# Transposes of x1 moved from TensorE to VectorE blocks and SBUF-to-SBUF transfers, with the order of a pass rearranged

## The chip, the cores and the metric

The kernel runs on one core of one Trainium2 chip. The metric is the device time of one execution in microseconds. Engines are named as in the profile: PE (TensorE), DVE (VectorE), ACT (ScalarE), POOL (GpSimd), SP (SyncE, which only issues transfers here).

## The reference

An input x of 2 x 4096 x 256 (float32) goes through one gated recurrence and one feed-forward block, each with a layer norm behind it:

```python
u = x @ W_in + b_in;  g = sigmoid(x @ W_gate + b_gate)
h_t = tanh(h_prev @ A + u_t @ Bm)            # a scan over 4096 steps
y_t = g_t * (h_t @ C.T + u_t @ D.T) + (1 - g_t) * x_t
x1  = layernorm(x + (y @ W_out + b_out + x))
h   = gelu(x1 @ bw1.T + b1)                  # 256 -> 1024, exact gelu
out = layernorm(x1 + (h @ bw2.T + b2))       # 1024 -> 256
```

bw1 and bw2 are the weights' signs times the mean magnitude of a row. The sums of the feed-forward block are kept exact to float32 by splitting x1 and h into a high part (float32r) and the remainder, `hi` and `lo`, and multiplying both with the signs.

## The kernel before, in words

Each of the two sequences is cut into 64 segments that run side by side (with 48 warm-up steps, and a comparison at the end that proves the segments' joints), so the recurrence takes 48 + 64 steps. A step is one product on PE and one tanh on ACT (`steps`, L156), strewn between the other work. The tokens are handled in 16 chunks of 512 (4 blocks of 128 tokens, 256 features).

The order of PE, ACT, DVE and POOL is written out by hand inside `tc.manual_schedule`: a sequence of `do(chunk, stage)` calls emits each stage's instructions on each engine, and an engine runs its own in that order. SP is not among these engines before, so its transfers are ordered by the compiler's scheduler.

A chunk goes through these stages:

- `load` (L342): its h and u are gathered from `st` into `hu` by two SBUF-to-SBUF transfers, its x into `xn`.
- `gate`, `tanh` (L357, L360): the gate's product, and a tanh on ACT into `tg`.
- `mix`, `mix_end` (L365, L380): the product `ps_y` on PE; POOL adds `b_out` to `xn` in four instructions (`add_row`, L353, with `bo_r`); DVE makes `d` (L377, L382) and then y in place of `tg` (L385).
- `project` (L388), in two halves: y times W_out on PE into `ps_z`; behind the second half DVE's addition into `xn`, which from here on is x1 (L406), and its statistics `bs_a`, `mv_a`, `rs_a`; POOL raises `rs_a` to the power -1/2 (L266).
- `shift`, `norm` (L410, L414): `nm_a` on DVE (L271), and the normalization in four instructions on ACT (L279).
- `turn` (L418): eight 128x128 transposes on PE into PSUM (`ps_t`, L423), `hi` copied by ACT (L431), `lo` subtracted by DVE (L433).
- `rest` (L437): POOL adds `b2` to x1 (L355, `b_r`).
- `up` g, for g = 0 to 3 (L442): eight products into two banks, two gelus (L458) and a rounded copy `hhi` (L467) on ACT. `low` g (L470): `hlo` on DVE (L474).
- `down` g (L532): 16 products with the second weights into `ps_o` (L490); behind g = 3 DVE scales it into `o` (L506).
- `add`, `stats`, `store` (L510 to L521): x1 + o on DVE (L512), statistics `bs_b`, `mv_b`, `rs_b`, POOL's power, normalization (L281, four instructions on DVE), and the transfer to `out`.

One pass c of the main loop (L723) works on several chunks, in this order on PE: up 0 of chunk c; down 2 of chunk c-1; mix of c+2; up 1; down 3 of c-1; a piece of the later chunks' gates (passes 1 to 12); turn of c+1; up 2; down 0; the first half of the projection of c+2; up 3; down 1; its second half. PSUM is full: three banks `h` for up and gates, two for `ps_y`, `ps_z` and `ps_t` in turn, two for `ps_o`, one for the recurrence. Tiles named with `bufs=` are reused in turn, and a reuse waits for the last reader.

Of the kernel before, what the change touches and what calls it, by code (L numbers as in the profile page):

```python
# [8 lines left out]
FP = mybir.dt.float32  # L9
FR = mybir.dt.float32r  # L10
# [6 lines left out]
P = 128  # L17
B, T, DM, S, H = 2, 4096, 256, 64, 1024
KD = DM // P
# [4 lines left out]
N = 512  # L24
# [3 lines left out]
TB = N // P  # L28
# [9 lines left out]
def gated_recurrence_then_binary_ffn(  # L38
# [16 lines left out]
    nc = tc.nc  # L55
# [3 lines left out]
    wk = ctx.enter_context(tc.tile_pool(name="work", bufs=2))  # L59
# [40 lines left out]
    def load_xT(c, pieces=1):  # L100
        x_tiles[c] = xp.tile([P, KD, N], FP, tag="xt", name=f"xt{c}", bufs=XTB)
        for k in range(pieces):
            cut = slice(k * KD // pieces, (k + 1) * KD // pieces)
            nc.sync.dma_start(out=x_tiles[c][:, cut, :], in_=xT[c][:, cut, :])
# [224 lines left out]
    class Chunk:  # L329


        def __init__(self, c, name, at=lambda a, c: a[c]):
            self.c, self.nm, self.at, self.xt = c, name, at, None

        def load_x(self):
            self.xt = xp.tile([P, KD, N], FP, tag="xt", name=f"xt_{self.nm}", bufs=XTB)
# [5 lines left out]
        def load(self):  # L342
            c, nm = self.c, self.nm
            self.hu = xp.tile([P, N], FP, tag="hu", name=f"hu{nm}", bufs=3)
            for r, src in (
                (TOP, h_of[:, bass.ds(c * SPC + 1, SPC)]),
                (LOW, u_of[:, bass.ds(c * SPC, SPC)]),
            ):
                nc.sync.dma_start(out=self.hu[r, :], in_=src.rearrange("p j b k -> p (j b k)"))
            self.xn = xp.tile([P, TB, DM], FP, tag="xn", name=f"xn{nm}", bufs=4)  # L350
            nc.sync.dma_start(out=self.xn, in_=self.at(x, c))

# [12 lines left out]
        def mix(self):  # L365

            nm, xt_ = self.nm, self.xt
            ps = p_m.tile([P, KD, N], FP, tag="m", name=f"ps_y{nm}")
            for m in range(KD):
                nc.tensor.matmul(  # L370
                    ps[:, m, :], cd[:, bass.ts(m, P)], self.hu, start=True, stop=True
                )
                if m < KD - 1:
                    yield
            self.add_row(self.xn, bo_r)
            self.d = wk.tile([P, KD, N], FP, tag="y", name=f"d{nm}", bufs=1)
            nc.vector.tensor_sub(self.d, ps, xt_)  # L377
            yield

# [38 lines left out]
        def turn(self, apart=False):  # L418
# [15 lines left out]
            self.h = {}  # L434
            yield

        def rest(self):  # L437

            self.add_row(self.x1, b2_r)
            yield  # L440

        def up(self, g, apart=False):  # L442
            nm = f"{self.nm}_{g}"
            h = wk.tile([P, 2, N], FP, tag="h", name=f"h{nm}")
            hi = wk.tile([P, 2, N], FR, tag="hhi", name=f"hhi{nm}", bufs=3)
            self.h[g] = h, hi
            for i in range(2):
                j = 2 * g + i
                ps = p_1.tile([P, N], FP, tag="h", name=f"ps_h{nm}_{i}")
                for n, (k, part) in enumerate((k, p) for p in (self.hi, self.lo) for k in range(KD)):  # L450
                    nc.tensor.matmul(  # L451
                        ps,
                        sg1[:, k, bass.ts(j, P)],
                        part[:, k, :],
                        start=n == 0,
                        stop=n == 2 * KD - 1,
                    )
                nc.scalar.activation(  # L458
                    h[:, i, :],
                    ps,  # L460
                    AF.Gelu,
                    bias=b1_c[:, j : j + 1],
                    scale=al1[:, j : j + 1],
                )
                if i == 1:
                    for part in range(2) if apart else [slice(0, 2)]:
                        nc.scalar.copy(hi[:, part, :], h[:, part, :])  # L467
                yield
# [41 lines left out]
        def add(self, blocks=range(TB), engine=nc.vector):  # L510
            cut = slice(blocks[0], blocks[-1] + 1)
            engine.tensor_tensor(  # L512
                self.x1[:, cut, :], self.x1[:, cut, :], self.o[:, cut, :], ALU.add
            )
            yield
# [68 lines left out]
        def redo(self):  # L584

            self.load_x()
            self.load()
            pieces = [self.gate, self.mix, self.mix_end, lambda: self.project(0), lambda: self.project(1)]
            pieces += [self.shift, self.norm, self.turn, self.rest]
            for g in range(KH // 2):  # L590
                pieces += [lambda g=g, f=f: f(g) for f in (self.up, self.low, self.down)]
            for piece in pieces + [self.add, self.stats, self.store]:
                for _ in piece():
                    pass


    ch = [Chunk(c, f"{c}") for c in range(NC)]
# [34 lines left out]
    def step():  # L632
        if ready():
            next_steps()

    def do(i, what, *args, pace=5600):
        if not 0 <= i < len(ch):
            return
        if what == "load":
            need = WARM + (ch[i].c + 1) * SPC  # L640
            while done < need:
                next_steps()
            ch[i].load()
        elif what in ("load_x", "load_gate_x"):
            getattr(ch[i], what)()
        else:
            emit(what, getattr(ch[i], what)(*args), pace)
# [4 lines left out]
        emit("part", (next(early, None) for _ in range(n)), pace)  # L652

    ET = mybir.EngineType
    with tc.manual_schedule(engines={ET.PE, ET.Activation, ET.DVE, ET.Pool}):
        waiting = []
        for c in range(FIRST + 1, FIRST + 6):
            load_xT(c)
# [5 lines left out]
        for n, pair in enumerate(pairs):  # L664
            before = 2 if n == 0 else 1
            parts(before, EARLY)
            if pair:
                emit("", u_of_chunks(*pair))
                if pair == (13, 14):
                    emit("", u_of_chunks(15, 0))  # L670
                emit("u", [None], EARLY)
            for c in loads[n]:
                load_xT(c)
            if n == 0:
                load_weights()
            if n == 3:
                halve_weights()
            if n >= 5:
                load_xT(n + 3)
            for i in range(7 - before):  # L680
                if 1 <= n < 5 and i == 0:
                    load_w(n - 1)
                if 2 <= n < 6 and i == 3:
                    prepare_w(n - 2)
                parts(1 if (n, i) != (6, 5) else 0, EARLY)
# [33 lines left out]
        end = len(ch) - 1  # L719
        parts_met = compare()  # L720
        since = -1 << 40
        late = gates(ch[10:], TB)
        for c in range(end):  # L723
            do(c + 6, "load_x")
            if c % 2 == 0:
                do(10 + c // 2, "load_gate_x")
            do(c, "up", 0)
            do(c, "low", 0)
            step()
            do(c - 1, "down", 2)  # L730
            do(c + 3, "load")
            if c > 0:
                do(c + 1, "shift")
                do(c + 1, "norm")
                do(c + 2, "mix")
                do(c + 2, "mix_end")
            do(c, "up", 1)
            step()
            do(c - 1, "down", 3)
            def add():  # L740
                do(c - 1, "add", range(TB), nc.gpsimd if c == end - 1 else nc.vector)
                if c < end - 1:
                    do(c - 1, "stats")

            if 1 <= c <= 12:
                add()
                emit("gate", (next(late, None) for _ in range(KD)))
            do(c + 1, "turn")
            do(c, "low", 1)
            if not 1 <= c <= 12:  # L750
                add()
            do(c + 1, "rest")
            do(c, "up", 2)
            do(c, "low", 2)
            if c == end - 1:
                do(c - 1, "stats")
            else:
                do(c - 1, "store")
            if c == end - 2:
                assert done == len(plan), done  # L760
                next(parts_met)
                next(parts_met)
            step()
            do(c, "down", 0)
            do(c + 2, "project", 0)
            do(c, "up", 3)
            step()
            do(c, "down", 1)
            do(c, "low", 3)
            if c == end - 1:  # L770
                do(c - 1, "store")
            do(c + 2, "project", 1)
            if c == end - 2:
                next(parts_met)
                next(parts_met)
        count()
        do(end, "up", 0)
        do(end, "low", 0)
        do(end - 1, "down", 2)
        do(end - 1, "down", 3)  # L780
# [76 lines left out]
```

## Time and profile before

| | |
|---|---|
| median of 3 runs | 451.37 us (451.14 to 454.42) |
| the profiled execution | 451.76 us |
| its span, first to last instruction | 450.0 us |
| mean granted TensorE clock | 0.994 |
| transfers issued by SP in one pass | 4 or 5 |

The span of the profile is cut from the first instruction to the last; what lies around it makes the 1.76 us to the execution's time. A row of a timeline is start, duration, engine, line, operation, output<-inputs and count; rows of the chain of work that ended last are start, duration, and what ran. "Idle before" names what the engine waited for. In rows of DVE two successive instructions may overlap by some 0.08 us[...].

The main loop's passes, by the chain: 23.41 us each for c = 1 to 10, 22.7 for c = 11 and 12 (the recurrence is over by then), 20.89 for c = 13 (no gate) and 17.45 for c = 14; chunk 15's own feed-forward takes the last 27.35 us.

### The profile page before, as it was taken

The page shows a single profiled execution, that of the slowest core. Times are in us where ns is not written, and L with a number is a line of the kernel's source. Part 1 is how long each engine was busy: PE and PEld are TensorE (multiplying, and loading weights), DVE is VectorE, ACT ScalarE, POOL GpSimd, SP SyncE. Part 2 cuts the span into 40 slices and gives each one's busy share as a digit, 9 for nine tenths or more (in the row PEclk, how much of TensorE's full clock was granted, in tenths as well). Part 3 has the DMA queues.
Part 4 walks back from the last instruction along what each step waited for, and adds up shares of the span by engine and source line. Part 5 has one row for each costly group of instructions (what it writes and reads, how often), then busy time and mean ns, then how long its engine had stood idle before and what let it go on. Part 6 is the DMA issues. An engine that isn't in the chain of part 4 may idle for free.

```text
span 450.0 us, 6729 instructions
## 1 busy us (share of the span) xinstructions
PE 438.2 (97%) x2506; PEld 355.6 (79%) x2506; DVE 357.4 (79%) x597; ACT 259.9 (58%) x424; POOL 177.6 (39%) x177
## 2 busy tenths in 40 slices
PE   8999999999999999999999999999999999999992
PEld 5665766788888888887979797979788888897982
DVE  0245927967979797989898889899898989887774
ACT  2443541585656574847474747566666656565771
POOL 1001300643545454545445454545454545433413
PEclk9999999999999999999999999999999999999997
DMA  8997824221133313331331313111202020201013
GB/s 298 306 320 289 290 67 134 69 86 23 48 108 104 108 58 106 105 106 58 105 106 61 105 60 105 61 58 50 70 20 87 1 93 1 93 1 48 1 47 101
DMA packets 14838, 44.51 MB, mean 99 GB/s; under 512 B 2000, under 2 KB 3024, under 8 KB 14800
## 3 DMA queue, kind: packets, MB, share of 16 engines
q1 hardware_dynamic: 14224, 43.65, 29.2%
q8 instruction: 22, 0.36, 0.4%
q10 hardware_dynamic: 576, 0.37, 0.3%
q14 instruction: 16, 0.13, 0.1%
HBM read 31.43 MB, written 8.39 MB: 88 GB/s over the span
## 4 chain that ended last, share of the span: by engine, by line
PE 86%; DVE 6%; DMA 3%; ACT 3%; issue 1%; POOL 1%; SPq 0%; POOLq 0%; DVEq 0%
PE ps_h L451 24%; PE ps_o L490 23%; PE ps_z L395 12%; PE ps_g L313 11%; PE ps_y L370 6%; PE ps_s L157 5%; PE ps_u L131 3%; PE ps_t L423 3%; DMA xt<-in_xT 3%; DVE hlo L474 1%; ACT xn L279 1%; ACT h L458 1%; DVE xn L281 1%; DVE bs_a L256 1%; ACT hhi L467 1%
## 5 line engine op out<-in xcount | busy, mean ns | idle before, releaser
L458 ACT ACTIVATE h<-ps_h,bias_c,al 128x512 f32<-128x512 f32 x128 | 97.4, 776 | 86.3 <-PE ps_h L451 80.3
L490 PE MATMUL ps_o<-sg,hhi 128*128 128x256 f32 x496 | 121.3, 285 | 0.0
L490 PE MATMUL ps_o<-sg,hlo 128*128 128x256 f32 x496 | 117.9, 279 | 0.1
L474 DVE TENSOR_TENSOR hlo<-h,hhi 128x1024 fp32r<-128x1024 f32 (+1 forms) x65 | 83.7, 1305 | 23.1 <-ACT hhi L467 23.0
L490 PEld LDWEIGHTS ps_o<-sg,hlo 128*128 128x128 f32 x496 | 93.5, 188 | 1.1 <-DVE hlo L474 0.3
L490 PEld LDWEIGHTS ps_o<-sg,hhi 128*128 128x128 f32 x496 | 93.5, 189 | 0.8
L451 PE MATMUL ps_h<-xhi,sg 128*128 128x512 f32 x256 | 91.8, 440 | 0.0
L355 POOL TENSOR_TENSOR xn<-xn,bo_r 128x256 f32<-128x256 f32 x64 | 65.4, 1052 | 48.4 <-DMA xn<-in_x 48.4
L451 PE MATMUL ps_h<-xlo,sg 128*128 128x512 f32 x256 | 80.1, 394 | 0.2
L355 POOL TENSOR_TENSOR xn<-xn,b_r 128x256 f32<-128x256 f32 x64 | 70.8, 1134 | 2.0 <-PE ps_t L423 2.0
L467 ACT CAST hhi<-h 128x1024 fp32r<-128x1024 f32 (+1 forms) x65 | 67.3, 1037 | 2.0
L313 PE MATMUL ps_g<-xt,w_gate 128*128 128x384 f32 (+3 forms) x208 | 66.3, 430 | 0.2 <-DMA xt<-in_xT 0.2
L266 POOL TENSOR_TENSOR rs_a<-rs_a,neg_half 128x4 f32<-128x4 f32 x16 | 17.2, 1075 | 121.3 <-DVE rs_a L265 96.6
L395 PE MATMUL ps_z<-w_out,tg 128*128 128x256 f32 x256 | 60.7, 380 | 0.0
L158 ACT ACTIVATE st<-ps_s 64x128 f32<-64x128 f32 x112 | 30.1, 269 | 47.6 <-PE ps_s L157 47.1
L451 PEld LDWEIGHTS ps_h<-xlo,sg 128*128 128x128 f32 x256 | 48.1, 188 | 11.8 <-DVE xlo L433 0.9
L451 PEld LDWEIGHTS ps_h<-xhi,sg 128*128 128x128 f32 x256 | 46.6, 189 | 13.4 <-issue 6.2
L157 PEld LDWEIGHTS ps_s<-st,wab 128*128 128x128 f32 x224 | 38.5, 188 | 22.2 <-ACT st L158 10.0
L266 POOL TENSOR_TENSOR rs_b<-rs_b,neg_half 128x4 f32<-128x4 f32 (+1 forms) x17 | 19.2, 1132 | 87.9 <-PE ps_s L157 49.9
L395 PEld LDWEIGHTS ps_z<-w_out,tg 128*128 128x128 f32 x256 | 46.1, 189 | 5.1
L279 ACT ACTIVATE xn<-xn,nm_a,rs_a 128x256 f32<-128x256 f32 x60 | 31.2, 591 | 26.5 <-DVE nm_a L271 26.5
L157 PE MATMUL ps_s<-st,wab 128*128 128x128 f32 x224 | 43.9, 278 | 0.1
(73 smaller groups left out, 483.5 us busy)
## 6 DMA issues: line engine op xcount, KB each, us to landing
xt<-in_xT SPq DMA_DIRECT2D x35, 512.0 KB, 4.2
xn<-in_x SPq DMA_DIRECT2D x16, 512.0 KB, 3.4
out_y<-xn SPq DMA_DIRECT2D x15, 512.0 KB, 2.6
hu<-st SPq DMA_DIRECT2D x32, 128.0 KB, 2.2
w1t<-in_w1T SPq DMA_DIRECT2D x2, 512.0 KB, 5.6
w1n<-in_w SPq DMA_DIRECT2D x2, 512.0 KB, 6.3
w2t<-in_w2T SPq DMA_DIRECT2D x2, 512.0 KB, 4.7
xt<-in_xT SPq DMA_DIRECT2D x2, 256.0 KB, 3.4
```

Source lines behind the costliest of these rows:

```text
L157: nc.tensor.matmul(p_h, ab, st[:, j].rearrange("p b k -> p (b k)"), start=True, stop=True)
L158: nc.scalar.activation(h_of[:, j + 1].rearrange("p b k -> p (b k)"), p_h[TOP, :], AF.Tanh)
L266: nc.gpsimd.tensor_tensor(rs, rs, neg_half[:, cut], ALU.pow)
L279: nc.scalar.activation(r, r, AF.Identity, bias=self.sh[:, i : i + 1], scale=rs)
L313: nc.tensor.matmul(ps[:, cut], w_gate[:, k, bass.ts(m, P)], xt_[:, k, cut], start=k == 0 and i == 0, stop=k == KD - 1, skip_group_check=True,)
L355: nc.gpsimd.tensor_tensor(r[:, i, :], r[:, i, :], row, ALU.add)
L395: nc.tensor.matmul(self.ps_z[:, i, :], self.y[:, k, bass.ts(i, P)], w_out[:, k, :], start=k == 0, stop=k == KD - 1,)
L451: nc.tensor.matmul(ps, sg1[:, k, bass.ts(j, P)], part[:, k, :], start=n == 0, stop=n == 2 * KD - 1,)
L458: nc.scalar.activation(h[:, i, :], ps, AF.Gelu, bias=b1_c[:, j : j + 1], scale=al1[:, j : j + 1],)
L467: nc.scalar.copy(hi[:, part, :], h[:, part, :])
L474: nc.vector.tensor_sub(lo[:, i, :], h[:, i, :], hi[:, i, :].bitcast(FP))
L490: nc.tensor.matmul(ps[:, i, :], part[:, j % 2, bass.ts(tb, P)], sg2[:, j, :], start=j == 0 and part is self.h[j // 2][0] and first, stop=j ...
```

## The change

For chunks 2 to 14 the transposes on PE are replaced: `blocks` turns x1 in 32x32 blocks by one DVE instruction into a new tile `xb`, and 16 SBUF-to-SBUF transfers on SP put the blocks in their places in `lo`. The tokens then stand in another order inside a chunk, which the gelu undoes as it writes h (a rearranged output). `split`, called between the two gelus of up 3 of the chunk before, makes `hi` (ACT) and the remainder `lo` (DVE, in place). Chunks 0, 1 and 15 keep `turn`.

The order of a pass changes as well. `shift` and `norm` of c+1 go to its head, then `low` 3 of c-1 (which stood at the end of the pass before), then `blocks`; `turn`, where it is left, keeps its place. Both halves of the projection of c+2 stand ahead of up 3, so its addition and statistics on DVE do too. The normalization of `store` is done by ACT (with a shift `nm_b` on DVE, as in `shift`), and stands between up 2 and `low` 2. `load` is split, with `load_n` for x; SP joins the engines whose order is written out by hand. `d` takes the buffer of `o`. In up 0 to 3 the products are as they were.

```diff
+        def blocks(self):
+            nm, Q = self.nm, P // 32
+            xb = wk.tile([P, DM // 32, TB, 32], FP, tag="xb", name=f"xb{nm}", bufs=1)
+            nc.vector.transpose(
+                out=xb, in_=self.x1.rearrange("p i (b r) -> p b i r", r=32)
+            )
+            self.lo = wk.tile([P, KD, N], FR, tag="xlo", name=f"xlo{nm}")
+            for a in range(Q):
+                for q in range(Q):
+                    nc.sync.dma_start(
+                        out=self.lo.bitcast(FP)[bass.ts(q, 32), :, bass.ts(a, P)],
+                        in_=xb[bass.ts(a, 32), q :: Q, :, :].rearrange("p k i c -> p k (i c)"),
+                    )
+            yield
+
+        def split(self):
+            self.hi = wk.tile([P, KD, N], FR, tag="xhi", name=f"xhi{self.nm}")
+            nc.scalar.copy(self.hi, self.lo.bitcast(FP))
+            nc.vector.tensor_sub(self.lo, self.lo.bitcast(FP), self.hi.bitcast(FP))
+            self.h = {}
+            self.far = True
...
-        def up(self, g, apart=False):
+        def up(self, g, apart=False, between=None):
...
+                to = h[:, i, :]
+                if self.far:
+                    to = to.rearrange("p (i a c) -> p a i c", a=P // 32, c=32)
                 nc.scalar.activation(
-                    h[:, i, :],
-                    ps,
+                    to,
+                    ps.rearrange("p (a i c) -> p a i c", a=P // 32, c=32) if self.far else ps,
...
+                if i == 0 and between is not None:
+                    between()
...
-    with tc.manual_schedule(engines={ET.PE, ET.Activation, ET.DVE, ET.Pool}):
+    with tc.manual_schedule(engines={ET.PE, ET.Activation, ET.DVE, ET.Pool, ET.SP}):
...
         for c in range(end):
+            far = 0 < c < end - 1
+            if c > 0:
+                do(c + 1, "shift")
+                do(c + 1, "norm")
+                do(c - 1, "low", 3)
+                if far:
+                    do(c + 1, "blocks")
+            do(c, "up", 0)
+            step()
+            do(c - 1, "down", 2)
+            if c > 0:
+                do(c + 2, "mix")
+                do(c + 2, "mix_end")
+            do(c, "low", 0)
+            do(c + 3, "load")
             do(c + 6, "load_x")
             if c % 2 == 0:
                 do(10 + c // 2, "load_gate_x")
-            do(c, "up", 0)
-            do(c, "low", 0)
-            step()
-            do(c - 1, "down", 2)
-            do(c + 3, "load")
-            if c > 0:
-                do(c + 1, "shift")
-                do(c + 1, "norm")
-                do(c + 2, "mix")
-                do(c + 2, "mix_end")
...
-            do(c + 1, "turn")
+            if not far:
+                do(c + 1, "turn")
...
             do(c, "up", 2)
+            if c < end - 1:
+                do(c - 1, "store", range(TB), nc.scalar)
+                do(c + 3, "load_n")
             do(c, "low", 2)
             if c == end - 1:
                 do(c - 1, "stats")
-            else:
-                do(c - 1, "store")
...
             do(c, "down", 0)
             do(c + 2, "project", 0)
-            do(c, "up", 3)
+            do(c + 2, "project", 1)
+            do(c, "up", 3, False, ch[c + 1].split if far else None)
             step()
             do(c, "down", 1)
-            do(c, "low", 3)
...
-            do(c + 2, "project", 1)
...
         do(end, "up", 0)
+        do(end - 1, "low", 3)
```

## The prediction

> **What bounds the kernel now.** I read the busy shares first, then the chain of work that ended last, then that chain inside one pass of the main loop, then DVE's and POOL's timelines beside it, and last SP's queue.
>
> ```profile
> PE 438.2 (97%) x2506; PEld 355.6 (79%) x2506; DVE 357.4 (79%) x597; ACT 259.9 (58%) x424; POOL 177.6 (39%) x177
> ```
>
> PE is busy nearly always; DVE has a fifth free on average, but not evenly. One pass of the main loop, from the chain:
>
> ```profile
> 221.79 1.85 PE ps_h L451 x8
> 223.64 0.22 PE ps_s L157 x2
> 223.86 1.83 PE ps_o L490 x16
> 225.70 1.72 PE ps_y L370 x4
> ...
> 231.31 1.72 PE ps_g L313 x4
> 233.03 0.87 PE ps_t L423 x8
> ...
> 245.20 0.94 PE ps_h L451 x4
> ```
>
> A pass is 245.20 - 221.79 = 23.41 us, all PE, with no wait in it. The eight transposes of `turn` are 0.87 us of it: the only PE work that the change takes away. In the table of stretches DVE is busy 20.93 us of these 23.41, so DVE has 2.5 us left. DVE's rows around it, then POOL's:
>
> ```profile
> 213.57 2.88 DVE L474 TENSOR_TENSOR hlo<-h,hhi 128x1024 fp32r<-128x1024 f32 x2
> 216.37 2.65 DVE L281 TENSOR_SCALAR xn<-xn,mv_b,rs_b 128x256 f32<-128x256 f32 x4
> ...
> 226.72 0.68 DVE L271 SCALAR_TENSOR_TENSOR nm_a<-mv_a,rs_a 128x4 f32<-128x4 f32 x1
> 227.45 1.23 DVE L377 TENSOR_TENSOR d<-ps_y,xt 128x1024 f32<-128x1024 f32 x1
> ...
> 250.12 0.16 DVE L271 SCALAR_TENSOR_TENSOR nm_a<-mv_a,rs_a 128x4 f32<-128x4 f32 x1
> ```
>
> ```profile
> 213.66 4.88 POOL L355 TENSOR_TENSOR xn<-xn,b_r 128x256 f32<-128x256 f32 x4
> ...
> 226.11 4.42 POOL L355 TENSOR_TENSOR xn<-xn,bo_r 128x256 f32<-128x256 f32 x4
> ```
>
> While POOL adds rows, a DVE instruction with two SBUF inputs takes longer: two `hlo` 2.88 instead of twice 1.22, `nm_a` 0.68 instead of 0.16. It works the other way too (DVE, then POOL, at the end of the run):
>
> ```profile
> 400.73 1.22 DVE L474 TENSOR_TENSOR hlo<-h,hhi 128x1024 fp32r<-128x1024 f32 x1
> ...
> 425.24 1.38 DVE L281 TENSOR_SCALAR xn<-xn,mv_b,rs_b 128x256 f32<-128x256 f32 x4 [0.91 <-POOL rs_b L266]
> ```
>
> ```profile
> 400.97 1.86 POOL L266 TENSOR_TENSOR rs_b<-rs_b,neg_half 128x4 f32<-128x4 f32 x1 [7.97 <-DVE rs_b L265]
> ```
>
> POOL's power, 1.02 elsewhere, came behind an `hlo` that ended at 401.95 and ended itself 0.88 later. And L281 x4 costs 1.38 with POOL idle, 2.65 beside its adds: the two engines take turns.
>
> **What the skill says.** "SBUF — State Buffer", section "Who interferes with whom": DVE instructions with two SBUF inputs and POOL instructions that read SBUF exclude one another for a whole instruction, and a DVE instruction with one SBUF input is free of it. The trace agrees: `d<-ps_y,xt` (one input in PSUM) stays at 1.23 beside POOL. "VectorE: DVE Perf Modes", section "The three transpose paths": DVE transposes within 32x32 blocks only, so the transfers must place the blocks. "Perfetto Trace Analysis", section "Identifying Dependency Chains": an instruction with many waits gets wait instructions in front of it; in this trace such ones stand 0.10 us apart.
>
> **The change, part by part.**
>
> *Taken away:* 0.87 us of PE in chunks 2 to 14, 13 x 0.87 = 11.3 us if PE stays the bound; L281 on DVE (2.65 a pass), which ACT does instead as in L279 (2.08 for four). ACT goes from 14.6 to 16.7 busy in a pass of over 22, which hides it; its `xhi` now reads SBUF, as `hhi` does (1.05 for 1.01).
>
> *DVE's transpose:* no row. The skill's "Vector Engine (DVE) Microarchitecture Reference", section 3.8, has one element per cycle and lane, so 1024 elements cost as the 1024-wide rows here: 1.22. It is issued behind `norm`, which ends near 2.5 us into a pass (`lo` at 0.27, `nm_a` 0.2, `norm` 2.08), and DVE's next, `d`, waits for `ps_y` until 5.66. Below 3.1 us it is free, above it every us counts.
>
> *16 transfers a chunk on SP:* nearest are the `hu` transfers, SBUF to SBUF:
>
> ```profile
> 63.66 1.13 SPq L349 DMA_DIRECT2D hu<-st  x2
> ```
>
> 0.58 apart, and 2.2 us to landing in the page's list. So 3.8 + 15 x 0.58 + 2.2 = 14.7 us into the pass, needed at about 20.8: free up to 0.98 us each. Bounds 0.33 (an `xt` load) to 1.2 (double); at 1.2 they come 3 us late. ACT's `xhi` waits for all of them, and behind it on ACT stand the second gelu of up 3, `hhi` 3 and the next `norm`. Behind the transfers on SP stand `hu`, `xt`, the store and `xn`, all with most of a pass to spare. `xn` waits for the store to land, and so lands some 2 us into the next pass; POOL's `bo_r` adds then run from 2.2 to 5.2, where DVE has nothing on the path.
>
> *The loop that closes.* Before, `hi` and `lo` of the next chunk were made in mid-pass, far ahead. Now `split` makes them inside the last up group; `lo`'s subtraction stands on DVE behind the projection's addition and statistics, and the next pass's up 0 needs it at its third matmul. PE then waits on DVE, and DVE's `d` on PE. I walk round this loop, times from start to start in the rows.
> 1. `lo` ends to `d` starts: `d` starts 227.45 - 221.79 = 5.66 behind up 0; `lo` must have ended 0.27 behind it (the row of the first `xlo` matmul stands at 222.10, less 0.04 for the signal). 5.39.
> 2. DVE without a gap: d 1.26, L382 1.26, L385 1.14, `hlo` 0 1.14, o 1.25, add 1.25, bs_b 1.33, mv_b 0.40, rs_b 0.08, `hlo` 1 1.22: 10.33. Everything these wait for is there earlier (the last is down 3, by 9.7 against `o` at 10.5).
> 3. The new `nm_b` stands between `hlo` 1 and `hlo` 2 and waits for POOL's power, which is shut out by `hlo` 1 and ends 0.90 behind it. POOL then starts its four b_r adds (0.75 alone); `nm_b` comes behind the first (0.75), `hlo` 2 behind the second (0.70) and runs 1.12. To the addition L410: 3.47.
> 4. L410 1.25, bs_a 1.33, mv_a 0.40, rs_a 0.45 (0.08 and four wait instructions for the 16 transfers), `lo` 1.22: 4.65.
> Sum 5.39 + 10.33 + 3.47 + 4.65 = 23.84, against 22.54 (23.41 - 0.87) for PE alone. PE then idles some 1.3 us a pass.
>
> *Sum over the run* (passes before from the chain): c = 1 to 10, 23.84 - 23.41 = 0.43, ten times 4.3. c = 11 and 12, where the recurrence is over: 23.62 (0.22 less in 1) against 22.70, twice 0.92 = 1.8. c = 13, without a gate, was 20.89 on PE; the DVE loop does not shrink, and the comparison adds 0.5: 24.1, so 3.2. c = 14 was 17.45 because the chain waited for the norm of chunk 15; now that comes first, and PE's own work is 4 x 3.67 + 0.87 + 0.12 = 15.7: -1.75. Start: the lower half of `hu` now follows the upper one in SP's order, 0.6 to 0.7 later in a chain that holds it: 0.7. Together +8.3: span 458.3 for 450.0, and for the median of 451.37 (the profiled execution took 451.76) **459.6 us**.
>
> **The rivals.**
> A. *POOL does not get in between* (it is late or early): step 3 is then 2.7, held by PE's projection at 18.67, and the loop is 23.05; with the same sum 10 x -0.36 + 2 x -0.07 + 2.0 - 1.75 + 0.7 = -2.8: 448.6. With `nm_b` alone delayed, the loop is 23.2 and the run about 450.7. Against it stands the taking of turns in the L281 rows; for it, that the order of two requests is decided within 0.1 us.
> B. *PE stays the bound*: all 11.3 of the transposes and the 1.75 come back, less 0.7: near 439. For it: a fifth of DVE is free on average, and DVE loses 2.65 and gains 1.22. It decides if `lo` is out by 0.27 us into a pass, which needs the loop at or below 22.54; my sum is 1.3 above it.
> C. *The transfers or the transpose are late*: at 1.2 us a transfer, or a transpose of 6 us, ACT and DVE wait 3 us a pass: 459.6 + 13 x 3 = 498; one us beyond the cover, 472.
> D. *Nothing moves*: the transposes gone, one stall of 0.87 in their place, 450 to 453, much as in A's second case.
>
> **How the numbers follow.** Forecast (459.6, own range 456 to 463) 0.56; A and D 0.24; B 0.09; C 0.11. About 1% (4.5 us) is what a measurement of this kernel tells from no change: faster means below 446.9, slower above 455.9. Slower holds the forecast and most of C: 0.65; same is most of A and D: 0.22; faster is B and the better edge of A: 0.13. The range runs from A's good end, 447.5, to the first late transfers, 465.
>
> **What would show it.** Right: PE waits in up 0 for `xlo` on DVE, about 1 us or more a pass, in passes 2 to 14; passes of 23.8 in the chain, with DVE in it from `d` to `xlo`; `nm_b` of 0.6 us or more and an `hlo` of 1.7 beside b_r; no gain in c = 11 to 13; pass 14 near 15.7. The transpose at 1.2 and the transfers landed by 15 us into a pass show the covered parts right. Wrong: passes of 22.5 with no wait for `xlo` (B), 23.0 with the `hlo` at 1.22 (A), ACT held at `xhi` by a transfer (C), or gelu writing its permuted rows much slower than 0.78, which I take as unchanged: up to 0.25 us more each has a us of cover at `xhi`.

## The result, and the profile after

The changed kernel takes 454.72 us (median of 7 runs, 453.23 to 456.27); the kernel before takes 451.76 beside it (7 runs, 451.14 to 454.42). The ratio is 1.0061, with a 95% interval of 1.0035 to 1.0088. The profiled execution of the changed kernel is its quickest: 453.23 us, with a span of 451.5. Against the span of 450.0 before, the sums below are made with these two: +1.5 us, where the prediction had +8.3.

The busy shares of the changed kernel, and the shares of its chain of work that ended last:

```profile
PE 430.5 (95%) x2402; PEld 344.3 (76%) x2402; DVE 332.3 (74%) x571; ACT 284.2 (63%) x476; POOL 158.9 (35%) x177
...
PE 40%; DVE 38%; issue 6%; POOL 5%; ACT 3%; SPq 3%; DMA 2%; DVEq 0%; POOLq 0%; ACTq 0%
```

PE lost 7.7 us of busy time and the span did not follow: the chain, all PE in a pass before, now runs through DVE for as long as through PE. One pass of the changed kernel from this chain (start, duration, what ran; in the changed kernel L381 is `d`, L507 `hlo`, L410 the projection's addition, L461 the remainder `xlo`):

```profile
203.92 1.24 DVE d L381
...
212.95 0.18 DVE rs_b L265
...
213.26 1.87 POOL rs_b L266
...
215.16 0.07 DVE nm_b L271
215.22 0.54 issue
215.76 1.21 DVE hlo L507
216.97 1.14 DVE xn L410
...
220.26 1.24 DVE xlo L461
221.50 0.04 issue
221.54 1.65 PE ps_h L479 x6
...
225.30 1.73 PE ps_y L374 x4
227.03 0.02 issue
227.06 1.24 DVE d L381
```

This is the loop that the prediction walked: `d`, the DVE chain, `xlo`, the third product of up 0, the mixture, the next `d`. It takes 227.06 - 203.92 = 23.14 us, not 23.84. Its middle is what the prediction argued about. Here is DVE's timeline in the changed kernel, then POOL's (the x4 are four adds in a row), then SP's for the transfers of the next chunk:

```profile
213.03 1.22 DVE L507 TENSOR_TENSOR hlo<-h,hhi 128x1024 fp32r<-128x1024 f32 x1
215.16 0.68 DVE L271 SCALAR_TENSOR_TENSOR nm_b<-mv_b,rs_b 128x4 f32<-128x4 f32 x1 [0.91 <-POOL rs_b L266]
215.76 1.21 DVE L507 TENSOR_TENSOR hlo<-h,hhi 128x1024 fp32r<-128x1024 f32 x1
216.90 1.21 DVE L410 SCALAR_TENSOR_TENSOR xn<-xn,ps_z 128x1024 f32<-128x1024 f32 x1
```

```profile
213.26 1.86 POOL L266 TENSOR_TENSOR rs_b<-rs_b,neg_half 128x4 f32<-128x4 f32 x1 [9.46 <-DVE rs_b L265]
215.10 3.87 POOL L359 TENSOR_TENSOR xn<-xn,b_r 128x256 f32<-128x256 f32 x4
```

```profile
225.02 11.29 SPq L452 DMA_DIRECT2D xlo<-xb  x16
```

POOL's power is shut out by the first `hlo` and takes 1.86; `nm_b` comes behind the first b_r add and takes 0.68. The second `hlo` does not wait: it runs its 1.21 at once. The second add alone, in POOL's timeline:

```profile
215.78 1.80 POOL L359 TENSOR_TENSOR xn<-xn,b_r 128x256 f32<-128x256 f32 x1
```

It starts 0.02 us behind the `hlo`, and it is the add that is held (1.80, where the first took 0.72).

To add up the run, each stage is taken from the third product of up 0 of one chunk to that of the next, in the traces of both:

| stage | before | after | difference | predicted |
|---|---|---|---|---|
| start, to chunk 1 | 105.07 | 106.01 | +0.94 | +0.7 |
| passes 1 to 10 | 234.15 | 231.58 | -2.57 | +4.3 |
| passes 11 and 12 | 45.39 | 45.74 | +0.35 | +1.8 |
| pass 13 | 20.88 | 24.53 | +3.65 | +3.2 |
| pass 14 | 17.67 | 16.09 | -1.58 | -1.75 |
| chunk 15 to the end | 26.84 | 27.55 | +0.71 | 0 |
| sum | 450.0 | 451.5 | +1.5 | +8.3 |

The miss is in passes 1 to 12: forecast to lose 6.1 us, they gained 2.2. A steady pass takes 23.13 us (before 23.41). Pass 9 took 23.50: DVE stood idle for 0.60 ahead of `xlo` there, in the pass shown above for 0.23, and the profile names the landing of a store as the end of that wait; why in this pass alone stayed open.

### The profile page after: what moved, and what is told of

The parts are those of the page before. It is cut to its first block, busy times and chain, and to the rows that moved or that the text cites. A ratio compares the mean times of both kernels' runs of the same rounds, so it can differ in the third digit from the quotient of the medians.

```text
span 451.5 us, 6834 instructions
## 1 busy us (share of the span) xinstructions
PE 430.5 (95%) x2402; PEld 344.3 (76%) x2402; DVE 332.3 (74%) x571; ACT 284.2 (63%) x476; POOL 158.9 (35%) x177
## 4 chain that ended last, share of the span: by engine, by line
PE 40%; DVE 38%; issue 6%; POOL 5%; ACT 3%; SPq 3%; DMA 2%; DVEq 0%; POOLq 0%; ACTq 0%
PE ps_o L523 8%; PE ps_h L479 8%; PE ps_g L313 7%; PE ps_y L374 6%; POOL rs_b L266 5%; DVE bs_b L256 4%; PE ps_s L157 4%; DVE xlo L461 4%; DVE d L386 4%; PE ps_u L131 3%; DVE bs_a L256 3%; DVE o L539 3%; DVE d L381 3%; DVE xn L545 3%; DVE tg L389 3%
## 5 line engine op out<-in xcount | busy, mean ns | idle before, releaser
L479 PE MATMUL ps_h<-xhi,sg 128*128 128x512 f32 x256 | 93.0, 445 | 0.5 <-ACT xhi L460 0.5
L479 PE MATMUL ps_h<-xlo,sg 128*128 128x512 f32 x256 | 81.5, 399 | 8.4 <-DVE xlo L461 8.2
L507 DVE TENSOR_TENSOR hlo<-h,hhi 128x1024 fp32r<-128x1024 f32 (+1 forms) x65 | 79.0, 1219 | 5.4 <-ACT hhi L500 5.3
L359 POOL TENSOR_TENSOR xn<-xn,bo_r 128x256 f32<-128x256 f32 x64 | 47.5, 774 | 84.8 <-DMA xn<-in_x 75.6
L266 POOL TENSOR_TENSOR rs_b<-rs_b,neg_half 128x4 f32<-128x4 f32 (+1 forms) x17 | 27.3, 1606 | 134.6 <-DVE rs_b L265 134.3
L359 POOL TENSOR_TENSOR xn<-xn,b_r 128x256 f32<-128x256 f32 x64 | 61.6, 993 | 2.0 <-PE ps_t L427 2.0
L399 PE MATMUL ps_z<-w_out,tg 128*128 128x256 f32 x256 | 58.2, 379 | 0.0
L279 ACT ACTIVATE xn<-xn,nm_b,rs_b 128x256 f32<-128x256 f32 x58 | 30.3, 594 | 40.1 <-DVE nm_b L271 40.1
L399 PEld LDWEIGHTS ps_z<-w_out,tg 128*128 128x128 f32 x256 | 47.2, 190 | 5.7
L381 DVE TENSOR_TENSOR d<-ps_y,xt 128x1024 f32<-128x1024 f32 x16 | 19.6, 1225 | 28.2 <-PE ps_y L374 28.2
```

The source lines that it names most:

```text
L266: nc.gpsimd.tensor_tensor(rs, rs, neg_half[:, cut], ALU.pow)
L359: nc.gpsimd.tensor_tensor(r[:, i, :], r[:, i, :], row, ALU.add)
L399: nc.tensor.matmul(self.ps_z[:, i, :], self.y[:, k, bass.ts(i, P)], w_out[:, k, :], start=k == 0, stop=k == KD - 1,)
L479: nc.tensor.matmul(ps, sg1[:, k, bass.ts(j, P)], part[:, k, :], start=n == 0, stop=n == 2 * KD - 1,)
L507: nc.vector.tensor_sub(lo[:, i, :], h[:, i, :], hi[:, i, :].bitcast(FP))
```

## The experiments

The theory at the start was the prediction's loop with a shorter third step: `xlo` gates up 0, PE makes the mixture, `d` waits for it, and DVE's chain leads to the next `xlo`. The rivals were other limits near 23.1 (DVE's own work, the transfers, PE), and the new order itself.

One thing lies across the times below. The granted clock is the share of its full clock that PE is given. In all 14 traces it was 1.00 in passes 1 to 12, so the length of a pass says more than a median. Outside these passes, and up to PE's last product, it fell in some traces to 0.5 for 3.4 or 6.8 us, each time around the end of a gap of 2.66 us or more in PE's work: 9 of 12 such gaps had it, the shorter ones (up to 1.73) never. A stretch of 3.4 us costs PE some 1.7 (an estimate: half of it). In pass 14, for example, PE worked without a gap for 16.09 us in the changed kernel (mean clock 1.00) and for 17.64 in one of the experiments below, the mixture moved (0.90).

**The order alone.** Every chunk is turned by PE; the rest of the new order stays.

```diff
-            far = 0 < c < end - 1
+            far = False
```

> All chunks turned by TensorE as before (no blocks, no transfers), everything else of the changed order kept. Theory (the changed kernel is held by a loop: xlo of one pass gates the third product of up 0, then the mixture, d, the DVE chain and the next xlo): with the turn on TensorE xlo hangs on no projection, so the loop is gone and TensorE alone sets the pass, 23.4 us for c = 1 to 10 and 22.7 for 11 and 12, as before; pass 13 falls from 24.5 to about 21; the time comes to 449 to 453, within 1% of the kernel before. Rival (the new order of the projection itself costs, by a wait of the addition and its statistics): passes over 23.6 and a time over 455 though the block transpose is gone.

Measured: 461.64 us, 1.018 times before (1.012 to 1.025). Passes 2 to 8 take 23.7 to 23.8, passes 11 and 12 23.2; pass 13 is 20.85, but pass 14 is 20.81 (16.09 in the changed kernel; PE has a gap of 3.07 in it, and a stretch of half clock behind that). The time is a miss; it fell on the rival's side. So by the medians the order costs about 10 us, and the blocks win some 7 of them back. The reason for the longer passes stands in this kernel's DVE timeline and chain, one line of each:

```profile
216.62 1.22 DVE L437 TENSOR_TENSOR xlo<-ps_t,xhi 128x1024 fp32r<-128x1024 f32 x1
```

```profile
217.90 3.71 PE ps_z L399 x16
```

`xlo` reads the turned chunk from PSUM, behind `o`, the addition and its statistics, and ends at 217.84. Only then does `ps_z`, which takes the same two banks, begin. This closes a loop of its own. To try this, the turn, and with it `xlo`, went ahead of the addition:

```diff
+            if not far:
+                do(c + 1, "turn")
             if 1 <= c <= 12:
                 add()
                 emit("gate", (next(late, None) for _ in range(KD)))
-            if not far:
-                do(c + 1, "turn")
```

> As the kernel with the order alone (all turns on TensorE), with the turn moved ahead of the addition and of the gate products, so that DVE's xlo, which reads the turned bank ps_t, comes before o, the addition and its statistics. Theory (in the order alone, the first product of the projection waited for xlo to free that bank: xlo ended at 217.84, the product began at 217.89, and so a loop of 23.78 runs through the bank, the mixture and the DVE chain): the loop is gone, TensorE alone sets the pass at 23.4 to 23.45, and the time falls from 461.6 by 4 to 6 to 456 to 457.5. Rival (the new order makes TensorE's own work longer, by its more waits): the pass stays at 23.7 to 23.8 and the time at 461 to 462.

Measured: 457.53 us, 1.014 (1.012 to 1.016), passes 23.43 (but 23.85 and 24.59 for 8 and 9) and 22.58 for 11 and 12. In the order alone PE's weight load for `ps_z` waited for `xlo` in each of passes 1 to 12 (3.8 us in all); here that wait is gone, and so are the longer passes: the bank's wait was the cause.

**Two cuts in the loop that bring nothing.** POOL's adds moved behind the projection:

```diff
-            do(c + 1, "rest")
             do(c, "up", 2)
...
             do(c + 2, "project", 1)
+            do(c + 1, "rest")
```

> The four b_r adds of POOL are moved behind the projection (so behind the power of rs_a), nothing else. Theory (nm_b behind the first b_r add is 0.5 us of the loop): nm_b takes 0.16 instead of 0.68, the second hlo and the addition start 0.5 earlier, the pass goes from 23.13 to about 22.63, and the time falls by about 6 to about 448.5. Rival (TensorE or the transfers set the pass, POOL is beside it): the pass stays at 23.1 and the time at 454 to 455.

Measured: 453.04 us, 1.0017 (0.9999 to 1.0035). `nm_b` takes 0.16 and the second `hlo` starts earlier, as expected, but the pass stays at 23.07 to 23.15 (two at 23.46 and 23.64).

The mixture moved ahead of down 2:

```diff
-            do(c - 1, "down", 2)
             if c > 0:
                 do(c + 2, "mix")
                 do(c + 2, "mix_end")
+            do(c - 1, "down", 2)
```

> The mixture of chunk c + 2 is put ahead of the first half of the last quarter of down products of chunk c - 1 (down 2), so 1.8 us of TensorE work leave the way from up 0 to d; nothing else. Theory (the loop through up 0, mixture, d and the DVE chain sets the pass): the loop shrinks by 1.0 to 1.8 to 21.3 to 22.1, below what TensorE needs alone (22.54), so the pass is 22.5 to 22.6 and xlo ends its gating; passes 11 to 13 gain about 1 each; the time falls by about 9 to 445 to 447. Rivals (DVE's own work and the waits between DVE and POOL set the pass, or the transfers do): the pass stays at 23.1 and the time at 454 to 455, d only waits longer behind its product.

Measured: 453.87 us, 1.0031 (1.0011 to 1.005), passes 23.11 to 23.22 (one 23.59). Both forecasts of a gain are misses: the loop was not the only limit. The chain of the kernel with the mixture moved says what took its place:

```profile
213.18 3.45 PE ps_z L399 x16
216.63 0.95 PE ps_h L479 x4
...
218.28 1.04 ACT xhi L460
219.32 0.69 ACT h L489
220.01 0.04 issue
220.05 1.24 DVE xlo L461
221.28 0.04 issue
221.33 1.65 PE ps_h L479 x6
```

The mixture and `d` are gone from it. PE runs without a gap from up 0 to the end of the projection at 216.63; L410 starts 0.04 behind that end in the trace, its statistics and four wait instructions end at 220.00, and `xlo` starts at 220.05. (The chain names ACT's gelu, which ends at 220.00 too; `xhi` was there at 219.32, and `rs_a`, the last of the statistics, ended at 219.81.) That L410 waits for the projection, and not for DVE's own work, shows in DVE's timeline of this kernel:

```profile
216.67 1.22 DVE L410 SCALAR_TENSOR_TENSOR xn<-xn,ps_z 128x1024 f32<-128x1024 f32 x1 [0.79 <-PE ps_z L399]
```

Only up 3 and down 1 lie on PE behind the projection, and they are shorter than L410 to `xlo`. In the changed kernel, too, the projection ends at 216.83 and L410 starts at 216.90: 18.47 us from the end of `xlo` (198.36), 0.07, and 4.60 from L410 to the next, again 23.14. New theory: two loops of one length, each hiding the other.

**The second loop cut alone, and both cut.** The projection went ahead of down 0:

```diff
-            do(c, "down", 0)
             do(c + 2, "project", 0)
             do(c + 2, "project", 1)
+            do(c, "down", 0)
```

> Both halves of the projection of chunk c + 2 are put ahead of down 0 (1.83 us of TensorE work leave the way to the end of the projection), nothing else. The pass stayed at 23.1 when the loop through the mixture was cut by the mixture's move, with xlo still gating up 0 behind L410, its statistics and four wait instructions that start with the end of the projection on TensorE. New theory (two loops of nearly one length: the first from xlo through the mixture and the DVE chain, 23.13; the second from xlo through all of TensorE's pass to the projection's end, then L410 to xlo, 23.1): this cuts the second loop to about 21.3 and leaves the first at 23.1, so the pass stays at 23.1 and the time at 453 to 456. Rival (the second loop alone sets the pass): the pass falls to 22.5 and the time to about 447.

Measured: 457.17 us, 1.0133 (1.0095 to 1.017), passes 23.16. The first loop alone makes 23.16. (Its span is 3.8 us above that of the changed kernel, but not by its steady passes: pass 0 takes 18.70 instead of 17.12, since `ps_z` waits 1.3 for `xlo` there, and pass 14 takes 18.57 instead of 16.09, with no gap in PE's work but a mean granted clock of 0.85 for 1.00.)

> Both moves together: the mixture ahead of down 2, and the projection ahead of down 0. New theory (two loops, each hiding the other): both are cut below 22.5, TensorE alone sets the pass at 22.5 to 22.6 for c = 2 to 10, 21.8 to 22.0 for 11 and 12, and the time falls by 6 to 9 to 445 to 448, though each move alone gives under 2. Rival (a third limit at 23.1, as the transfers on SP's queue or DVE's own work): the pass stays at 23.1 and the time at 452 to 455.

Measured, with both moves: 448.23 us, 0.9911 (0.988 to 0.9942), passes 22.57 and 21.8. Its chain has nothing but PE in these passes; four successive lines around the places where DVE stood before:

```profile
220.84 1.89 PE ps_o L523 x16
222.73 1.87 PE ps_h L479 x8
224.60 0.22 PE ps_s L157 x2
224.82 1.72 PE ps_y L374 x4
```

By itself neither move changed a steady pass by more than some 0.05 us; together they take 0.56 off it. In the medians one gained 0.9 us and the other lost 2.5 (pass 0 and the clock, as above); together they gain 6.5. A third limit at 23.1 is excluded, since neither DVE's work, nor the transfers, nor POOL's adds were changed.

**What `nm_b` costs when nothing hides it.** POOL's adds behind the projection once more, this time with the projection ahead of down 0:

```diff
-            do(c + 1, "rest")
             do(c, "up", 2)
...
             do(c + 2, "project", 0)
             do(c + 2, "project", 1)
             do(c, "down", 0)
+            do(c + 1, "rest")
```

> The projection is ahead of down 0 (as in the kernel whose pass was 23.16 by the loop through the mixture alone) and the b_r adds of POOL are behind it, so nm_b has no add ahead of it. Theory (two loops; nm_b behind the first b_r add is 0.5 us of the first): with the second loop cut, these 0.5 us now come through: the pass is 22.6 to 22.7 for c = 2 to 10, 0.5 below the 23.16 of the projection's move alone, and the time is 5 to 7 below its 457.2, at 450 to 452. Rival (POOL's adds cost the loop nothing, as their removal alone seemed to say): the pass stays at 23.1 to 23.2, the time at 456 to 458.

Measured: 449.87 us, 0.9974 (0.9947 to 1.0), passes 22.55 to 22.63. The same edit that brought nothing now brings 0.55 a pass, down to PE's own limit: the wait of `nm_b` was in the first loop.

**The prediction's third step, turned.** One idle copy of `nm_b` was put ahead of the second `hlo`:

```diff
+            if far:
+                tip = sm.tile([P, TB], FP, tag="tip", name=f"tip{c}")
+                nc.vector.tensor_scalar(tip, ch[c - 1].st2.sh, 1.0, None, ALU.mult)
             do(c, "low", 2)
```

> One more small DVE operation (a 128x4 copy of nm_b to a tile of its own, read by nobody) ahead of the hlo that follows nm_b, nothing else. In the changed kernel this hlo started 0.02 us ahead of the second b_r add. Theory of the prediction (hlo has to wait for the second b_r add where that comes first): the small operation waits for the second b_r add (0.7) or hlo does, and perhaps for the third (0.7 more): the pass goes from 23.13 to between 23.9 and 24.7, the time up by 8 to 17 to 463 to 472. Rival (hlo doesn't wait for POOL's adds at all, the order within 0.02 us means nothing): the operation costs its own 0.1 to 0.16, the pass 23.3, the time at most 457.

Measured: 463.75 us, 1.024 (1.018 to 1.030), passes 23.82: 0.69 for an operation of some 0.16. Its DVE timeline, and then the third of POOL's adds there:

```profile
217.45 0.68 DVE L271 SCALAR_TENSOR_TENSOR nm_b<-mv_b,rs_b 128x4 f32<-128x4 f32 x1 [0.91 <-POOL rs_b L266]
218.17 0.66 DVE L802 TENSOR_SCALAR tip<-nm_b 128x4 f32<-128x4 f32 x1
218.74 1.21 DVE L507 TENSOR_TENSOR hlo<-h,hhi 128x1024 fp32r<-128x1024 f32 x1
```

```profile
218.76 1.79 POOL L359 TENSOR_TENSOR xn<-xn,b_r 128x256 f32<-128x256 f32 x1
```

The copy waits for the second add (0.66), as I had thought `hlo` would, and the `hlo` behind it is again 0.02 ahead of POOL's next add. The copy reads a single SBUF tile, so having one SBUF input did not free it. With this wait in it the pass is 23.82, where the prediction had 23.84. With the stages as in the table above, passes 1 to 10 cost +3.75 (predicted +4.3) and 11 and 12 +1.70 (+1.8).

**The cover of the transfers.** `xhi` went to the place behind the `hhi` of up 2, `xlo` behind `nm_b`, so both ahead of the addition:

```diff
             do(c, "up", 2)
+            if far:
+                ch[c + 1].upper()
             if c < end - 1:
                 do(c - 1, "store", range(TB), nc.scalar)
+                if far:
+                    ch[c + 1].split()
...
-            do(c, "up", 3, False, ch[c + 1].split if far else None)
+            do(c, "up", 3)
```

Here `upper` holds the ACT half of `split`, and `split` the DVE half.

> The two halves of chunk c + 1 are split before the addition instead of behind it: xhi on ACT right behind the hhi of up 2 (where ACT idled 2.7 us), xlo on DVE behind nm_b and ahead of the third hlo and of L410; nothing else moves. Theory (both loops end in xlo behind L410 and its statistics): xlo leaves both, TensorE sets the pass at 22.5 to 22.6, and c = 13 falls from 24.5 to 25 to 20 to 22, since the late addition of that pass no longer holds up 0; the time falls by 8 to 12 to 443 to 447. Rival (the blocks arrive too late for this: x1 waits for nm_a, the transpose and 16 transfers, 14.7 us after xlo): xhi waits for transfers, ACT's queue behind it with it, and the pass is 23 or more, the time 452 or more.

Measured: 467.54 us, 1.034 (1.031 to 1.037), passes 2 to 10 of 23.0 to 24.9. The rival was right. This kernel's chain:

```profile
221.91 1.86 DMA xlo<-xb
...
224.03 1.06 ACT xhi L460
...
225.12 1.23 DVE xlo L463
226.34 1.14 DVE hlo L509
227.48 1.14 DVE xn L410
...
234.04 1.26 DVE xb L446
...
246.05 1.85 DMA xlo<-xb
```

With L410 queued behind `xlo`, the transpose, the 16 transfers and the landing come into a loop: 13.9 us from the transpose's start to the last landing, 24.1 from one last landing to the next. In the changed kernel these lie beside other work.

**Passes 13 and 14.** Chunk 14 was turned by PE:

```diff
-            far = 0 < c < end - 1
+            far = 0 < c < end - 2
```

> Chunk 14 is turned by TensorE, as chunk 15 is, the other twelve as in the changed kernel. Theory of the prediction (pass 13 costs 3.6 more than before because xlo of chunk 14 stands behind that pass's DVE chain): pass 13 has no xlo behind the addition, and goes from 24.5 to about 21.5, TensorE gets 0.87 back for the turn; the time falls by 2 to 3 to about 452. Rival (pass 13's DVE chain is the limit whoever turns the chunk, as it seems in the kernel with the order alone, whose pass 13 took 24.8): the pass stays at 24 to 25 and the time at 454 to 455.

Measured: 454.21 us, 1.0066 (1.0032 to 1.01), no change. (The order alone took 20.85 in pass 13, not 24.8 as the rival has it.) Pass 13 did fall to 20.99, but pass 14 rose from 16.09 to 20.85: 3.0 of it is a gap in which PE waits for a gelu, and some 1.7 the half clock behind the gap (0.92 in the mean). The chain of this kernel there:

```profile
408.57 2.07 ACT xn L279 x4
410.64 0.67 ACT h L489
411.31 0.04 issue
411.36 1.43 PE ps_h L479 x4
```

The gelu of up 0 stands on ACT behind the normalization of chunk 15, which waits for the late DVE chain of pass 13 as `xlo` did. So I kept this edit and both moves, and in pass 14 put `shift` and `norm` behind up 0:

```diff
             if c > 0:
-                do(c + 1, "shift")
-                do(c + 1, "norm")
+                if c < end - 1:
+                    do(c + 1, "shift")
+                    do(c + 1, "norm")
...
+            if c == end - 1:
+                do(c + 1, "shift")
+                do(c + 1, "norm")
             do(c, "low", 0)
```

> Both moves (mixture ahead of down 2, projection ahead of down 0), chunk 14 turned by TensorE, and in pass 14 nm_a of chunk 15 and its four normalizations on ACT put behind up 0, whose gelu waited behind them. Theory: passes 2 to 12 as with both moves (22.57 and 21.9); in passes 13 and 14 up 0 of chunk 14 hangs on the late DVE chain no more, so the two together fall from 39.6 by 1 to 2 to about 38; the time is 446 to 447.5, against 448.2 with both moves alone. Rival (the late DVE chain of pass 13 holds the end whatever stands where, since chunk 15's turn waits for it): no change from 448.2.

Measured: 443.59 us, 0.9832 (0.9814 to 0.985), better than I expected and the fastest of all: passes 13 and 14 take 21.62 and 15.88, passes 2 to 10 22.57. With both moves alone these two had taken 23.51 and 17.54, so they fell by 3.55 and not by 1 to 2. What the forecast lacked is the clock: with both moves PE had a gap of 2.7 us at the end of pass 13 and a mean clock of 0.91 in pass 14, worth some 1.7; here the gap is gone and the clock is 1.00. All five runs had a mean clock of 0.994 to 0.996, the four with both moves alone 0.985 to 0.989. Its busy shares:

```profile
PE 427.8 (97%) x2410; PEld 346.1 (78%) x2410; DVE 336.9 (76%) x570; ACT 284.0 (64%) x476; POOL 166.3 (38%) x177
```

Last, the same order with all turns on PE (`far = False`, the turn ahead of the addition as above):

> As the fastest kernel so far (both moves, the late norm of chunk 15), but all chunks turned by TensorE, ahead of the addition and the gate products: no blocks, no transfers. Theory (once TensorE alone sets the pass, the turn is worth its 0.87 us of TensorE in each of the 12 passes that lose it): passes of 23.4 to 23.5 for c = 2 to 10 and 22.7 for 11 and 12, and a time 10 to 11 above the 443.6, at 453.5 to 455. Rival (the gain lies in the order of the last passes, and the blocks give little): a time of 444 to 448.

Measured: 453.75 us, 1.0026 (0.9997 to 1.0055), passes 23.46 and 22.6. In this order the blocks are worth 10.2 us, a turn's 0.87 in each of 12 passes (in the traces, 10.5 over passes 1 to 12).

## Why the prediction was wrong in size

The loop and its place were right; the forecast of +8.3 was several times what came (+1.5 in the profile, +3.0 in the medians). The direction came out right by luck: where the loop was forecast to cost 6.1 us, in passes 1 to 12, the run got 2.2 faster, and only the other stages made it slower.

- *Step 1*, 5.39: measured 5.56 (`xlo` ends 198.36, `d` starts 203.92). *Step 2*, 10.33: measured 10.33. *Step 4*, 4.65: measured 4.60, the wait instructions included.
- *Step 3* failed: "`nm_b` comes behind the first (0.75), `hlo` 2 behind the second (0.70) and runs 1.12 ... 3.47". It took 2.65. The power and `nm_b` waited as said; `hlo` 2 came 0.02 us ahead of the second add and ran 1.21. The mis-sized term is this 0.70, which measured 0; twelve passes of it are 8.4 us, and these passes missed by 8.3. (The rest of the step came 0.12 shorter as well, and step 1 0.17 longer.) The kernel with the idle copy put the wait back, and the pass became 23.82. The price of the wait was right; who has to wait was not.
- *Why this term was wrong.* I took from the two `hlo` of the kernel before (2.88 together) that DVE and POOL take turns. The Trainium skill ("SBUF — State Buffer", section "Who interferes with whom") says more: issue order decides who blocks. The traces agree. In the kernel before the add started at 213.66, inside the first `hlo`, and the second `hlo` at 214.70, so the add went first and the `hlo` took 1.75:

```profile
214.70 1.75 DVE L474 TENSOR_TENSOR hlo<-h,hhi 128x1024 fp32r<-128x1024 f32 x1
```

In the changed kernel the order is 215.76 for `hlo`, 215.78 for the add, so `hlo` went first. The rows of before could have told this, by an argument that was not tested by itself: DVE's next row starts some 0.08 ahead of the end of the one before, POOL's only 0.03 (`rs_a` ends at 226.14, the bo_r adds start at 226.11). In the changed kernel `nm_b` ends 0.02 behind the first add (215.84 and 215.82), which puts DVE's next at 215.76 and POOL's at 215.78, as measured.

- *Rival A* named what happened, "with `nm_b` alone delayed, the loop is 23.2", and its sign, an `hlo` of 1.22 (measured 1.21). It also named the second limit ("held by PE's projection at 18.67"; measured 18.47). I used it as a floor of that case only and missed that it stands within 0.05 us of the first loop. It made no difference to the forecast, but to what an engineer would try next: each cut alone fails.
- *The start* (+0.94 for 0.7), *pass 13* (+3.65 for 3.2) and *pass 14* (-1.58 for -1.75) came near what was worked out. That pass 13 suffers through `xlo` is only part of it: with `xlo` taken away the late chain shows up in pass 14, by a gap of 3.0 and the half clock behind it.
- *The covered parts* held: the transpose 1.25 for 1.22; the last transfer landed 16.1 us after `xlo` for 14.4 (14.7 into the pass), as the pitch was 0.70 on average and not 0.58, still 4 us ahead of `xhi`. The move of the normalization to ACT and gelu's permuted writing (0.78) cost the loop nothing.
- *Rival B* was 22.54 for a pass; PE's own need is indeed 22.57, and two moves reach it. *Rival C* did not come in the changed kernel; moving `xlo` forward brought its wait about.

Open: the 0.71 us behind chunk 15; single passes of 23.5 to 24.6 around pass 9, of which the two in the order with the turn moved have the store's normalization on ACT, and behind it the recurrence's tanh, in their chain; the start, where the `hu` of chunk 1 landed 2.2 us after its issue in the changed kernel's profile and 3.6 to 4.0 in those of three experiments with the same beginning, two of which had half clock behind it; and why the clock falls behind some gaps and not behind others. A part of the spread between runs is this clock: the twelve runs of the kernel with the projection and POOL's adds moved go from 447.89 us at a mean of 0.994 to 454.41 at 0.985.

## What to carry to other kernels

When an engine gets work taken away and the time doesn't follow, list every loop that leads back to the gated instruction, not only the one that the chain shows: two loops of equal length hide each other, and only cutting both shows either. Where two engines exclude each other, set the start times of both down to hundredths, since the first to arrive goes first; where that can't be told, both outcomes get their chance. A stage that is moved behind a late chain on one engine will be late on the next engine too, so move its followers as well. And set the granted clock beside each stage before its length is put down to a wait.

## What the runs showed of the hardware

How close an order can be and still be steady: in all 13 passes of the changed kernel that have it, and in all 13 of that with the idle copy, a 128x1024 DVE operation came 0.015 to 0.023 us ahead of POOL's add (215.76 against 215.78, 218.74 against 218.76). A small DVE operation that arrives during a POOL add costs most of the add (0.66 to 0.68 for some 0.16), while the large one behind it cost nothing but its own time and made POOL wait (1.80 for 0.72). An idle copy of 128x4, with one SBUF input, thus cost 0.69 us a pass.

Long gaps in PE's work mostly came with a slower clock: at 9 of the 12 gaps of 2.66 to 3.97 us the granted clock fell to 0.5 for 3.4 or 6.8 us around the gap's end, at none of those of up to 1.73 us. With the gap of 2.7 us that pass 13 had with both moves, pass 14 took 17.54; without it, 15.88.
